# A four-layer hybrid on one core: layer 0's convolution, outputs and query weights rearranged, and a new order at layer 3's end

## The chip, the cores and the metric

The kernel runs on one core of a Trainium2 chip. The core has a matrix engine (TensorE, PE in the profile; its weight loads are listed apart as PEld), VectorE (DVE), ScalarE (ACT), GpSimd (POOL) and SyncE (SP); each works through its own queue in order, and they wait for each other by semaphores. DMA transfers are issued from the queues of SP, ACT and POOL. The metric is the device time of one execution in microseconds (us). All data are float32 unless said otherwise.

## What is computed

An input of 4 images, 256 channels, 32 x 32 pixels goes through four layers. As tokens it is 4 x 1024 rows of 256 numbers. Cut to what matters here, with `B = 4` images, `L = 1024` tokens and `D = 256` channels:

```python
# layer 0: a state-space block with an attention over channels
u = layernorm(x_tokens) * norm_g + norm_b
z, xBC, dt = split(u @ in_w.T);  dt = softplus(dt + dt_bias)
xBC = silu(causal_conv4(xBC) + conv_b);  xs, Bm, Cm = split(xBC)
state_t = state_{t-1} * exp(-dt_t * exp(A_log)) + (dt_t * xs_t) Bm_t;   y_t = state_t Cm_t
y = (y + Dp * xs) * silu(z);  y = y * rsqrt(mean(y*y) + EPS) * rms_w
out = y @ out_w.T                                   # 256 x 256
pooled = mean(out over the image's tokens)
attn = sigmoid(relu(pooled @ se1_w.T + se1_b) @ se2_w.T + se2_b)
x = x + out * attn                                  # attn per image and channel
# layer 1: three 1-channel projections theta, phi, g of x; their product, batch norm, added to x
# layer 2: full attention (one head of 256) over each image, then 2 of 8 experts (256 -> 1024 -> 256)
q = h @ Wq + bq;  k = h @ Wk + bk;  t = t + softmax(q k^T / 16) (h @ Wv + bv)
# layer 3: lam = softmax_tokens(h @ W_k)^T (h @ W_v + b_v), batch norm of lam, t + (h @ W_q + b_q) lam;
#          then an LSTM of 1024 steps over the 4 images; its outputs are added to t
```

silu(v) is v times sigmoid(v), which equals (v/2) (1 + tanh(v/2)).

## The kernel before

The kernel is one program in Bass with the Tile framework. Outside of the blocks `tc.manual_schedule`, the framework's planner chooses the order of the instructions on each engine from the program order and from its own idea of when inputs are ready; so instructions of different images stand among each other in the trace, and some that need only a constant input stand far ahead of their place in the code. `tc.keep_in_program_order(x)` ties an instruction behind the one traced before it on its engine; `tc.issue_after(x)` ties what a block traces on x's engine behind x. Inside a manual block the code's order is the order.

**Layer 0, projection** (`_project`). The tokens come in 8 blocks of 512, two an image. `load` fetches a block, turns it by matmuls with `turner` (L246; the matrix also holds the three weights of layer 1, whose products go to `of_x`), takes the layer norm's moments and scales. `turn` turns it back, `project` multiplies with the weights: z and dt (L276) and the four groups of 128 of xBC, `xbc[b]` (L284, copied by ACT at L287). After an image's second block `convolve(b)` does, for each group `m`, one ACT operation (L294), three DVE multiply-adds of 128x1024 (L299) and a silu on ACT (L302). After the last block `_decays` computes dt and the decay factors of all images: exponent, logarithm, the exponent of A_log (L349), three matmuls with triangular matrices and their exponents (L356). Image 3's `convolve` comes after it. The weights of layer 0 come in one DMA, `w_l0` (in the profile w_l); its part w_out is scaled by rms_w at L201.

**Layer 0, scans** (`_scan`, `_out`). An image has 8 chunks of 128 tokens. A chunk transposes its xBC (ptr, L375), copies it (xb, L378), builds the decay matrix (au L386, pd L388, m_h L390 and L391), multiplies (py L397, pst L406 and L411), updates the state on DVE (L413, L414) and multiplies y with silu(z) into `zs` (L417); ACT sums the squares (L419). `_out(b)` then takes the square root's inverse (rstd, L432, POOL), turns the scaled rows by matmuls with diagonal matrices (L443) into `yT` with sums over tokens (L447), multiplies the sums with w_out (L456), with se1 (L464) and se2 (L468), and takes the sigmoid by tanh (L471). With the attention it scales w_out (`w_att`, L474), gets three more columns by six products summed over channels (`junk`, L478), and multiplies yT with it, chunk by chunk (L486): the 256 columns are added to `s.rows` (L489), the other three go to `of_y` (L490). The code's order is scan 0, scan 1, out 0, scan 2, out 1, scan 3, out 2, out 3. [...]

**Layer 1** (`_layer1`) is a chain of small operations on of_x and of_y, and ends with l1_row (L555). **Layer 2** (`_layer2_attention`) loads its weights w_l2 (L128, also w_l in the profile), folds the query and key weights into one matrix, `m_qk` and `b_qk` (L592 to L602), and then norms image 0's rows (L620, L138, L158), and so on. The experts (`_layer2_experts`) follow; beside the early tiles `_lstm_constants` loads and halves the LSTM's weights (L1474).

**Layer 3's end** (`_layer3_first`, in a manual block). For the first 128 tokens of every image it computes q (L1348, L1353), runs three products that nothing reads (L1360), norms lam (L1416, L1419), multiplies (`p_u`, L1439), adds (L1422), norms, turns (L1434) and copies the result to `u3_first`, the LSTM's first input. Between, `other()` computes products of w_q and lam (`matrices`, L1375) that later tokens need: one of two halves for images 0 to 2. The fourth image's two halves are left to `s.rest[0]`, which `_layer3_lstm` runs in its step t = 0, after that step's own matmuls. A step injects the inputs (L1651), multiplies the state (L1708), and goes through DVE and ACT (L1719 to L1747).

Of the kernel before, what the change touches and what calls it, by code (L numbers as in the profile page):

```python
# [18 lines left out]
P = 128  # L19
B = 4  # L20
# [40 lines left out]
    "norm_g": 2, "norm_b": 2, "conv_w": 16, "conv_b": 4, "rms_w": 2, "se1_b": 1,  # L61
# [64 lines left out]
def _weights(s, name):  # L126
    w = s.wpool.tile([P, C, NW[name]], F32, name=name, tag="w")
    s.nc.scalar.dma_start(w, s.d[name].rearrange("(k p) n -> p k n", p=P))  # L128
    return w
# [40 lines left out]
def _layer0_and_1(s):  # L170
# [5 lines left out]
    with ExitStack() as ctx:  # L176
# [5 lines left out]
        wide = keep.tile([P, 5, D], F32, name="wide")  # L182
        nc.scalar.dma_start(
            wide.rearrange("p i d -> p (i d)"), s.d["wide"].to_broadcast([P, 5 * D])
# [4 lines left out]
            three=wide[:, 2:, :],  # L189
# [10 lines left out]
        for k in range(C):  # L200
            nc.vector.tensor_scalar_mul(  # L201
                v.w_out[:, k, :], v.w_out[:, k, :], s.col["rms_w"][:, k : k + 1]
            )
        _project(s, v, keep)
        v.dt, v.decay, v.total, v.tail = v.decays
        with ExitStack() as body:
            pools = SimpleNamespace(
                scan=body.enter_context(tc.tile_pool(name="ssm", bufs=2)),
                out=body.enter_context(tc.tile_pool(name="out", bufs=2)),
                ps=body.enter_context(tc.tile_pool(name="ssm_ps", bufs=2, space=PSUM)),  # L210
            )
            for b in range(B):
                _scan(s, v, pools, b)
                if b > 0:
                    _out(s, v, pools, b - 1)
            _out(s, v, pools, B - 1)
# [3 lines left out]
def _project(s, v, keep):  # L220
# [4 lines left out]
    with ExitStack() as ctx:  # L225
# [5 lines left out]
        for k in range(C):  # L231
            nc.vector.tensor_copy(turner[:, k, 3:], s.ident)
            for j, name in enumerate(("theta_w", "phi_w", "g_w")):
                nc.vector.tensor_copy(turner[:, k, j : j + 1], s.col[name][:, k : k + 1])
        held = {}
# [53 lines left out]
        def convolve(b):  # L289
            for m in range(NXBC):  # L290
                x = v.xbc[b][:, m, :]
                acc = pool.tile([P, L], F32, name="acc")
                tap = s.col["conv_w"][:, m * DCONV : (m + 1) * DCONV]
                nc.scalar.activation(  # L294
                    acc, x[:, off:], AF.Identity,
                    bias=s.col["conv_b"][:, m : m + 1], scale=tap[:, off:],
                )
                for j in range(off):
                    nc.vector.scalar_tensor_tensor(  # L299
                        acc, x[:, j : j + L], tap[:, j : j + 1], acc, ALU.mult, ALU.add  # L300
                    )
                nc.scalar.activation(x[:, off:], acc, AF.Silu)  # L302
# [4 lines left out]
        for i in range(NBLK):  # L307
# [7 lines left out]
            if i % BPI == BPI - 1:  # L315
                convolve(i // BPI)


def _decays(s, keep, pool, ps, dtr):
# [29 lines left out]
    nc.scalar.activation(na, s.row["A_log"], AF.Exp)  # L349
# [11 lines left out]
def _scan(s, v, pools, b):  # L361
# [5 lines left out]
    state = pool.tile([P, NH, HD], F32, name="state")  # L367
    for c in range(TPI):
        n = b * TPI + c
        t = slice(off + c * P, off + (c + 1) * P)  # L370
        bT, cT = xbc[:, 2, t], xbc[:, 3, t]

        ptr = ps.tile([P, 4, P], F32, name="ptr")
        for m in range(3):
            nc.tensor.transpose(ptr[:, m, :], xbc[:, m, t], s.ident)  # L375
        nc.tensor.matmul(ptr[:, 3, :], bT, cT, start=True, stop=True)
        xb = pool.tile([P, 3, P], F32, name="xb")
        nc.scalar.copy(xb, ptr[:, :3, :])  # L378
        gm = pool.tile([P, P], F32, name="gm")
        nc.vector.tensor_mul(gm, ptr[:, 3, :], s.upper)  # L380
        xh = xb[:, :2, :].rearrange("p c (h d) -> p (c h) d", d=HD)


        au = pool.tile([P, NH, P], F32, name="au")
        for h in range(NH):
            nc.scalar.mul(au[:, h, :], s.upper, a[:, n, h : h + 1])  # L386
        pd = ps.tile([P, NH, P], F32, name="pd", bufs=1)
        nc.tensor.matmul(pd, s.lower, au, start=True, stop=True)  # L388
        m_h = pool.tile([P, NH, P], F32, name="m_h")
        nc.scalar.activation(m_h, pd, AF.Exp)  # L390
        nc.vector.tensor_mul(m_h, m_h, _bc(gm, 1, NH))  # L391

        xdt = pool.tile([P, NH, HD], F32, name="xdt")
        nc.gpsimd.tensor_mul(xdt, xh, _bc(v.dt[:, n, :], 2, HD))
        py = ps.tile([P, NH, HD], F32, name="py", bufs=1)
        for h in range(NH):
            nc.tensor.matmul(py[:, h, :], m_h[:, h, :], xdt[:, h, :], start=True, stop=True)  # L397

        y = pool.tile([P, NH, HD], F32, name="y")
        nc.gpsimd.tensor_mul(y, xh, _bc(s.row["Dp"], 2, HD))  # L400
        nc.vector.tensor_add(y, y, py)
        xw = pool.tile([P, NH, HD], F32, name="xw")
        nc.gpsimd.tensor_mul(xw, xh, _bc(v.tail[:, n, :], 2, HD))
        pst = ps.tile([P, 2, NH, HD], F32, name="pst")
        if c > 0:
            nc.tensor.matmul(pst[:, 0], cT, state, start=True, stop=True)  # L406
            y_in = pool.tile([P, NH, HD], F32, name="y_in")
# [1474 lines left out]
```

## Time and profile before

| | us |
|---|---|
| median of 3 runs | 3427.09 (3426.97 to 3430.27) |
| the profiled execution | 3423.79 |
| its span | 3422.0 |
| layer 0, first matmul to the last of_y | 7.28 to 340.6 |
| layer 1, to l1_row | 340.6 to 348.0 |
| layer 2, attention | 348.0 to about 708 |
| experts | about 708 to 1210 |
| layer 3 to u3_first | about 1240 to 1344 |
| LSTM | 1344 to the end |

All times of single instructions are those of the one profiled execution and count from its span's start. The profile gives, for each engine, busy times, the idle time before an instruction and what ended it ("<-"); a matmul of float32 appears as two passes, so a product over 256 rows of 256 columns is four passes. The chain that ended last is followed back from the last instruction of the program to what released each step.

### The profile page before, as it was taken

Reading aid. Unit: us, or ns where it says so; the run is one execution under the profiler, and the core shown is the slowest. Engines: PE = TensorE matmul, PEld = TensorE weight load, DVE = VectorE, ACT = ScalarE, POOL = GpSimd, SP = SyncE. Lnnn points to the kernel's source line nnn. Section 1 sums busy time; section 2 is a strip of 40 time slices with the busy share of each in tenths; the row PEclk is TensorE's granted clock in tenths of the full one; section 3 lists DMA queues with packets and bytes.
Section 4 is the critical chain, followed back from the end, with each engine's and each line's share of the span. In section 5 each row is a group of like instructions: output and inputs, shape, how many; then the busy total and the mean of one; then the engine's idle time right before and its main releaser. Section 6 shows DMA issues by size and latency. Waiting matters only on the chain.

```text
span 3422.0 us, 143796 instructions
## 1 busy us (share of the span) xinstructions
PE 3104.9 (91%) x63646; PEld 2493.8 (73%) x63646; DVE 1837.6 (54%) x8224; ACT 1099.1 (32%) x4347; POOL 529.4 (15%) x746
## 2 busy tenths in 40 slices
PE   8797899999999989998998998998998998998887
PEld 5476577678888856777777777777777777777776
DVE  5785644651111143565555565555665665555555
ACT  5763222222222222332332332332332332332222
POOL 2252100124444320001001001001001001001000
PEclk9898999999999999999999999999999999999999
DMA  2000011246666620000000000000000000000000
GB/s 82 1 1 1 10 38 38 102 152 213 194 198 210 199 61 1 4 4 10 4 4 10 4 4 10 4 4 10 4 4 10 4 4 10 4 4 9 5 4 10
DMA packets 49220, 140.65 MB, mean 41 GB/s; under 512 B 4944, under 2 KB 38032, under 8 KB 43856
## 3 DMA queue, kind: packets, MB, share of 16 engines
q0 software_dynamic: 18768, 101.03, 9.5%
q1 hardware_dynamic: 27680, 24.45, 2.2%
q8 instruction: 499, 8.18, 1.0%
q10 hardware_dynamic: 2144, 5.95, 0.5%
q14 instruction: 129, 1.06, 0.1%
HBM read 106.18 MB, written 25.22 MB: 38 GB/s over the span
## 4 chain that ended last, share of the span: by engine, by line
PE 54%; DVE 26%; ACT 11%; issue 6%; POOL 2%; DMA 1%; ACTq 0%; DVEq 0%; SPq 0%; POOLq 0%
PE pre L1708 16%; DVE col L1719 11%; PE ph L1204 7%; PE po L1213 7%; PE pre L1651 6%; ACT tri L1722 5%; DVE scan L1731 5%; DVE hs L1742 4%; PE p_a L1605 3%; PE p_w L768 3%; PE p_s L734 3%; DVE acc L299 1%; PE p_o L486 1%; PE p_d L1309 1%; PE p_w L755 1%
## 5 line engine op out<-in xcount | busy, mean ns | idle before, releaser
L1708 PE MATMUL pre<-w_v,hs 128*4 128x64 f32 x49104 | 872.8, 219 | 207.4 <-DVE hs L1742 196.8
L1708 PEld LDWEIGHTS pre<-w_v,hs 128*4 128x4 f32 x49104 | 684.1, 86 | 395.6 <-DVE hs L1742 393.7
L1651 PE MATMUL pre<-xg,pick 128*128 128x64 f32 x6144 | 903.9, 283 | 0.5 <-DVE xg L1618 0.5
L1651 PEld LDWEIGHTS pre<-xg,pick 128*128 128x128 f32 x6144 | 763.5, 191 | 118.1 <-DVE xg L1618 0.9
L1719 DVE STREAM_TRANSPOSE col<-pre 128x64 f32<-128x64 f32 x2048 | 484.0, 250 | 304.2 <-PE pre L1708 289.3
L1722 ACT ACTIVATE tri<-col 128x16 f32<-128x16 f32 x1024 | 229.9, 225 | 1173.5 <-DVE col L1719 1173.5
L1731 DVE TENSOR_TENSOR_SCAN scan<-tri 128x24 f32<-128x24 f32 x1024 | 216.3, 211 | 361.0 <-ACT tri L1722 361.0
L1613 POOL TENSOR_TENSOR xg<-xg,gate_bias 128x192 f32<-128x192 f32 x127 | 75.0, 590 | 1602.9 <-ACT xg L1612 1602.9
L1204 PE MATMUL ph<-xT,wt 128*128 128x256 f32 (+1 forms) x1184 | 253.7, 370 | 1.6 <-issue 0.9
L1207 ACT ACTIVATE hT<-ph,wt 128x256 f32<-128x256 f32 (+1 forms) x296 | 136.9, 463 | 353.6 <-PE ph L1204 346.6
L1213 PE MATMUL po<-wt,hT 128*128 128x256 f32 x1120 | 248.9, 379 | 0.0
L1204 PEld LDWEIGHTS ph<-xT,wt 128*128 128x128 f32 x1184 | 205.6, 189 | 41.6 <-ACT hT L1207 6.2
L1213 PEld LDWEIGHTS po<-wt,hT 128*128 128x128 f32 x1120 | 209.9, 190 | 27.0
L1740 DVE STREAM_TRANSPOSE gate<-row 128x64 f32<-128x64 f32 x1024 | 228.2, 223 | 0.7
L1729 ACT ACTIVATE row<-pre 128x64 f32<-128x64 f32 x1024 | 210.5, 206 | 0.6
L1747 DVE SCALAR_TENSOR_TENSOR tri<-hs,scan 128x8 f32<-128x8 f32 x1023 | 181.6, 178 | 36.1 <-DVE hs L1742 1.5
L1182 DVE COPY xT<-p_x 128x512 f32<-128x512 f32 (+1 forms) x37 | 24.5, 662 | 205.7 <-PE p_x L1178 205.6
L1224 DVE TENSOR_TENSOR y<-po,wt 128x256 f32<-128x256 f32 x70 | 29.6, 424 | 186.0 <-PE po L1213 185.9
L1605 PE MATMUL p_a<-w_u,u 128*32 128x192 f32 x1792 | 119.3, 338 | 0.0
L734 PE MATMUL p_s<-u,q 128*128 128x512 f32 x256 | 117.0, 596 | 0.0
L768 PE MATMUL p_w<-v,prT 128*128 128x256 f32 x512 | 116.0, 379 | 0.7 <-ACT prT L760 0.7
L768 PEld LDWEIGHTS p_w<-v,prT 128*128 128x128 f32 x512 | 95.5, 190 | 15.5 <-issue 2.9
(2462 smaller groups left out, 3284.0 us busy)
## 6 DMA issues: line engine op xcount, KB each, us to landing
xn<-xn SPq DMA_DIRECT2D x8, 516.0 KB, 3.6
x<-in_x_dram SPq DMA_DIRECT2D x16, 256.0 KB, 3.1
acc<-rows SPq DMA_DIRECT2D x8, 512.0 KB, 2.9
out_dram<-part SPq DMA_DIRECT2D x64, 64.0 KB, 1.7
xn_early<-xn SPq DMA_DIRECT2D x6, 516.0 KB, 5.0
rows<-acc SPq DMA_DIRECT2D x6, 512.0 KB, 8.3
w_l<-in_w_l_dram ACTq DMA_DIRECT2D x1, 1092.0 KB, 9.5
rows<-acc SPq DMA_DIRECT2D x4, 256.0 KB, 4.2
```

Source lines behind the costliest of these rows:

```text
L734: nc.tensor.matmul(p[:, h, :], v.q[:, k, bass.ts(j, P)], v.u[:, k, bass.ts(h, W)], start=k == 0, stop=k == C - 1,)
L768: nc.tensor.matmul(p, prT[:, n, :], images[g // TPI].v[:, n, :], start=n == 0, stop=n == TPI - 1)
L1204: nc.tensor.matmul(ph, w1[:, k, bass.ts(m, P)], xT[:, k, :], start=k == 0, stop=k == C - 1)
L1213: nc.tensor.matmul(po, hT[:, m, bass.ts(j, P)], w2[:, m, :], start=m == 0, stop=m == NHC - 1)
L1605: nc.tensor.matmul(p[32 * j : 32 * (j + 1), :], u3[i * SG // P][:, k, bass.ts(i % (P // SG), 32)], w_u[:, k, j * Q : (j + 1) * Q], start=k ...
L1651: nc.tensor.matmul(p, pick[:, r].rearrange("p j r -> p (j r)"), xg[i][:, v], start=True, stop=t == 0,)
L1708: nc.tensor.matmul(p[32 * j : 32 * j + B, :], hs[:, t - 1, k * B : (k + 1) * B], w_v[:, k, j * Q + v.start : j * Q + v.stop], start=False, ...
L1719: nc.vector.transpose(col[:, g * C : (g + 1) * C, :].rearrange("p n r -> p (n r)"), pre[t % 2][g])
L1722: nc.scalar.activation(z[:, 2:50].rearrange("p (g q) -> p g q", g=2)[:, :, ::3].rearrange("p g (k b) -> p (g k) b", k=C), col[:, :, :B], A ...
L1729: nc.scalar.activation(row, pre[t % 2][2], AF.Tanh)
L1731: nc.vector.tensor_tensor_scan(scan, z[:, 0 : 3 * S], z[:, 26 : 26 + 3 * S], 0.0, ALU.mult, ALU.add)
L1740: nc.vector.transpose(gate.rearrange("p n r -> p (n r)"), row)
```

## The change

Layer 0. Image 3's convolution is taken out of `_project` and done in four parts after chunks 0, 2, 4 and 6 of scan 0, with silu as tanh and one more DVE operation; its accumulators have a pool of their own. The scaling of w_out, its transpose `out_t` and the product `w_in` of w_out and se1 are made once, after scan 0's last chunk. `_out` is split: `_attention(b - 1)` is in the code after chunk 1 of scan b, `_out(b - 1, j)` after chunks 4 to 7, two each, and for b = 3 one each. Image 2's other four outputs are tied behind products of image 3's attention. yT lies in xbc[b]'s first two groups. The three columns come from a product of out_t with the theta, phi and g weights times the attention, not from `junk`. w_l2 is loaded after the projection, and m_qk and b_qk are computed at the end of layer 0. The exponent of A_log and L1474's scalings are kept in program order.

Layer 3's end. No products that nothing reads; the second half of q is made by DVE; all four images' lam are scaled first, then the four p_u, then all eight matrices between the adds and the turns; the LSTM's step 0 has no such product any more.

The diff, cut to its core:

```diff
-        for k in range(C):
-            nc.vector.tensor_scalar_mul(
-                v.w_out[:, k, :], v.w_out[:, k, :], s.col["rms_w"][:, k : k + 1])
-        _project(s, v, keep)
-        v.dt, v.decay, v.total, v.tail = v.decays
-        with ExitStack() as body:
...
+        with tc.tile_pool(name="conv", bufs=2, side="right") as conv, ExitStack() as body:
+            _project(s, v, keep, conv)
+            v.dt, v.decay, v.total, v.tail = v.decays
+            s.w_l2 = _weights(s, "w_l2")
+            tc.keep_in_program_order(s.w_load)
...
             for b in range(B):
-                _scan(s, v, pools, b)
-                if b > 0:
-                    _out(s, v, pools, b - 1)
-            _out(s, v, pools, B - 1)
+                for c in range(TPI):
+                    _scan(s, v, pools, b, c)
+                    if b == 0 and c % 2 == 0:
+                        _convolve_last(s, v, pools, conv, c // 2)
+                    if b == 0 and c == TPI - 1:
+                        _out_weights(s, v, pools)
+                    if b > 0 and c == 1:
+                        held = _attention(s, v, pools, b - 1)
+                    if b > 0 and c >= TPI // 2:
+                        n = 1 if b == B - 1 else 2
+                        for j in range(n * (c - TPI // 2), n * (c - TPI // 2 + 1)):
+                            _out(s, v, pools, b - 1, j, held, "p_o")
+            beside = [
+                lambda j=j: _out(s, v, pools, B - 2, j, held, "ptr") for j in range(TPI // 2, TPI)
+            ]
+            last = _attention(s, v, pools, B - 1, beside)
+            for j in range(TPI):
+                _out(s, v, pools, B - 1, j, last, "ptr")
+            _query_weights(s, pools.ps)
...
-            if i % BPI == BPI - 1:
+            if i % BPI == BPI - 1 and i + 1 < NBLK:
                 convolve(i // BPI)
+def _convolve_last(s, v, pools, conv, m):
+    nc = s.nc
+    if m == 0:
...
+        nc.gpsimd.tensor_scalar_mul(v.half_w, s.col["conv_w"], 0.5)
+        nc.gpsimd.tensor_scalar_mul(v.half_b, s.col["conv_b"], 0.5)
+    acc = _convolution(s, v, conv, B - 1, m, v.half_w, v.half_b)
+    dst = v.xbc[B - 1][:, m, DCONV - 1 :]
+    nc.scalar.activation(dst, acc, AF.Tanh)
+    nc.vector.scalar_tensor_tensor(dst, dst, 1.0, acc, ALU.add, ALU.mult)
...
-    nc.scalar.activation(na, s.row["A_log"], AF.Exp)
+    tc.keep_in_program_order(nc.scalar.activation(na, s.row["A_log"], AF.Exp))
...
+def _out_weights(s, v, pools):
+    nc, pool, ps = s.nc, pools.out, pools.ps
+    for k in range(C):
+        s.tc.keep_in_program_order(nc.vector.tensor_scalar_mul(
+            v.w_out[:, k, :], v.w_out[:, k, :], s.col["rms_w"][:, k : k + 1]))
...
+            nc.tensor.transpose(p[:, bass.ts(k, P)], v.w_out[:, k, bass.ts(m, P)], s.ident)
+        nc.scalar.copy(v.out_t[:, m, :], p[:, :D])
...
+def _attention(s, v, pools, b, beside=()):
...
+    def fill(product):
+        if beside:
+            with s.tc.issue_after(product.ins):
+                beside.pop(0)()
...
-    yT = pool.tile([P, C, L], F32, name="yT", bufs=1)
+    yT = v.xbc[b][:, :C, DCONV - 1 :]
...
+    for k in range(C):
+        mm = nc.tensor.matmul(
+            p, v.w_in[:, k, :], pooled[:, k : k + 1], start=k == 0, stop=k == C - 1)
+    fill(mm)
...
+    mine = pool.tile([P, C, 3], F32, name="mine")
+    nc.vector.tensor_mul(mine, v.three, _bc(att[:, D:], 2, 3))
...
-            nc.vector.scalar_tensor_tensor(
-                junk, w[:, k, :D], 1.0, v.three[:, j, :], ALU.mult, ALU.mult,
...
 def _layer3_first
+    p_q = [ps.tile([P, W], F32, name="p_w") for _ in range(C)]
...
-    p = ps.tile([P, W], F32, name="p_w")
-    for _ in range(3):
-        nc.tensor.matmul(p, s.ident, u[:, 0, :W], start=True, stop=True)
...
-    between = [matrices(b, [m]) for b in range(B - 1) for m in range(C)]
+    between = [matrices(b, [m]) for b in range(B) for m in range(C)]
...
     for b in range(B):
         scaled(b)
+        if b == 1:
+            nc.vector.tensor_scalar_add(
+                q[:, 1].rearrange("p b t -> p (b t)"), p_q[1], s.col["b_q"][:, 1:2])
+    for b in range(B):
         for k in range(C):
             nc.tensor.matmul(p_u[b // 2][:, b % 2, :], q[:, k, b, :], lam[:, k, b, :],
...
-        if b < B - 1:
-            other()
-        if b > 0:
-            added(b - 1)
-    normalised(0, B // 2)
-    added(B - 1)
+    added(0)
+    added(1)
+    rstd = _rstd(s, pool, moments[:, : B // 2, :])
+    added(2)
+    _scaled(s, un[:, : B // 2, :], mine[:, : B // 2, :], moments[:, : B // 2, :], rstd)
+    added(3)
     normalised(B // 2, B)
-    other()
-    other()
+    for _ in range(5):
+        other()
...
     turned(0, B // 2)
-    other()
+    for _ in range(3):
+        other()
     turned(B // 2, B)
...
-    s.rest = [matrices(B - 1, list(range(C)))] + [bias(b) for b in range(B)]
+    s.rest = [bias(b) for b in range(B)]
...
-        nc.vector.tensor_scalar_mul(io, io, 0.5)
+        s.tc.keep_in_program_order(nc.vector.tensor_scalar_mul(io, io, 0.5))
...
             if t == 0:
-                p = aside()
-                mm, out = lambda: s.rest[0][0](p), lambda: s.rest[0][1](p)
+                pass
```

`_query_weights` is L592 to L602 of before with two PSUM tiles of the tag p_o; `_convolution` is L294 to L299; `_out` is one chunk of L486 to L490.

## The prediction

> **What bounds the kernel now.** I read the page first, then the windows of layer 0, then the chain that ended last and the timeline in the four places that the diff touches.
>
> The page gives the span, and PE as the fullest engine. The loops that carry the chain (LSTM steps L1708 to L1747, experts L1204 and L1213) aren't edited; they hand any shift on one for one.
>
> ```profile
> span 3422.0 us, 143796 instructions
> PE 3104.9 (91%) x63646; PEld 2493.8 (73%) x63646; DVE 1837.6 (54%) x8224; ACT 1099.1 (32%) x4347; POOL 529.4 (15%) x746
> ```
>
> Windows of layer 0's second half: stretch, length, busy time and count of PE, PEld, DVE, ACT, POOL, then PE clock. The first two are the scans of images 0 and 1 (the py matmuls, eight a chunk, count 71 and 60). PE is the limit with DVE just behind it; in the last row PE works 30 of 43 us at clock 0.76.
>
> ```profile
> 152.00:183.00 31.00, 30.66 (x163) 22.96 (x163) 24.36 (x60) 25.56 (x76) 16.57 (x26) 0.91 0.01 2
> 183.00:213.00 30.00, 27.61 (x158) 20.04 (x158) 28.05 (x64) 21.42 (x65) 20.28 (x29) 1.00 0.00 1
> 260.00:298.00 38.00, 36.17 (x196) 29.32 (x196) 31.27 (x87) 20.25 (x66) 12.67 (x19) 0.91 0.00 1
> 298.00:341.00 43.00, 30.04 (x124) 22.88 (x124) 16.49 (x61) 7.28 (x30) 2.14 (x5) 0.76 0.00 0
> ```
>
> The timeline of the start: DVE, in order, sits on two operations whose DMAs are late (the bias scaling L1474, the w_out scaling L201), and PE waits behind each.
>
> ```profile
> 6.67 0.43 DVE L1474 TENSOR_SCALAR rows<-rows 128x512 f32<-128x512 f32 x1 [2.14 <-DMA rows<-in_rows_dram]
> 7.28 2.12 PE L246 MATMUL p_x<-turner,x 128*128 128x131 f32 x8 [7.28 <-DVE turner L232]
> 11.26 0.62 DVE L201 TENSOR_SCALAR w_l<-w_l,cols 128x256 f32<-128x256 f32 x2 [3.89 <-DMA w_l<-in_w_l_dram]
> ```
>
> The timeline before the first scan: DVE convolves image 3, and the first chunk's xb is copied only at 149.97.
>
> ```profile
> 142.31 6.44 DVE L299 SCALAR_TENSOR_TENSOR acc<-xbc,cols,acc 128x1024 f32<-128x1024 f32 x5
> 149.97 0.48 ACT L378 COPY xb<-ptr 128x384 f32<-128x384 f32 x1
> ```
>
> The chain at the end of layer 0 (start, length): image 2's outputs stand ahead of image 3's turned rows, and its own outputs come after another attention.
>
> ```profile
> 308.51 10.48 PE p_o L486 x32
> 318.99 3.81 PE p_o L443 x32
> 328.67 1.14 DVE junk L478 x6
> 329.94 10.03 PE p_o L486 x32
> ```
>
> The chain at layer 3's end: three filler products (six passes), four rounds of ACT lam then p_u, and after the first LSTM step a product of eight passes that the second step waits for.
>
> ```profile
> 1326.08 2.58 PE p_w L1360 x6
> 1337.27 1.15 PE p_u L1439 x4
> 1343.47 0.59 ACT u_first L1462
> 1348.70 3.52 PE p_a L1375 x8
> 1352.22 0.78 PE pre L1708 x48
> ```
>
> **What the Trainium skill says.** "TensorE: Matmul & The Clock Gate", section "What's actually happening", halves the clock after an idle window of some 3.4 us. The trace agrees: after PE's wait that ended at 308.5 the first passes of L486 come at 0.37 us, later ones at 0.2. "SBUF — State Buffer", section "Who interferes with whom", says that a DVE operation with two SBUF inputs and a GpSimd one that reads SBUF exclude each other. The trace agrees: m_h L391 takes 674 to 1139 ns, and y L409 took 0.83 where POOL's xw ran beside it, else 0.42. "ScalarE: Activation LUTs", section "What ACT_TABLE_LOAD costs", prices a load at 1283 ns; all eight loads before the first chunk show 1.28.
>
> **The change part by part**, in us of the profiled execution (span 3422.0; that run took 3423.79, 1.8 around the span).
>
> 1. *Start.* L1474 and L201 go to later places, and so does the exponent of A_log with a table load (7.04 to 8.53 on ACT). Turner can follow its columns at about 5 instead of 7.28, if x has landed (2.8 us at best from issue at 0.8): −1.5. PE's second stop, 9.4 to 12.0, goes: −2.6. w_l lands at 11.2, ahead of the first p_z (then about 15). From 20 on PE is busy 18 to 19 of every 20 us, so the shift stays: **−4** (−5 to −2). POOL's three new copies run while it is idle (2.6 to 15.4); the w_l2 load costs ACT one issue of 0.38.
>
> 2. *Image 3's convolution moves into scan 0.* The decays then need dtr (125.6), two tables, twelve small DVE operations and three matmuls: about 135, so the chunks start 15 earlier. DVE gets twelve operations of 1.28 in the scan plus four new ones (the product with 1+tanh), also 1.28: 20.5. Against that, scan 0's DVE work is 24 and its PE work 28. Some 4 of the 20.5 fit ahead of 135; the rest makes 24 + 16.5 = 40.5, at about 92% full 44: ends at 179, where scan 0 ends now (about 180). What PE gains at the front it loses to DVE: **0**. Bounds: −12 if the extra work sinks into later DVE gaps; +6 if the shared port stretches it. Tanh beside Exp needs no new load (none shows after 153.18 although L471 is a tanh). Two silu table loads go, inside the 15.
>
> 3. *Scans 1 to 3.* Before 298 PE now also gets image 2's attention (2.2) and four of its outputs (4 x 0.86 = 3.4): 5.6, at 93% full **+6**. The other sixteen outputs were in the scans before. Eight L456 passes (1.05) per image give way to about as many narrow ones; twelve junk operations of 0.35 leave DVE. The w_out scaling and transposition (about 2.5 on PE) fall in scan 0, where DVE is the limit: nothing, 2.5 if that cover is gone. Bounds 0 to +14.
>
> 4. *Tail.* From the last zs (297.2) to the last of_y (340.6) are 43.4 now. After: rstd 3.0; turned rows at first at half clock, about 7, and last yT 0.8; pooled, w_in, hdn 1.2; se2 and two fillers, att, tanh 3.4; mine, out_t and a filler, w_att 2.0; eight outputs at 0.9, 7.2, and 0.8 to the copy: 25.4. **−18** (−22 to −14). Image 2's last four outputs are in it as fillers (0.86 each); if they push each DVE step behind a 0.42 rows add, that is the 14.
>
> 5. *Query weights.* 2.5 of PE at full clock now follow the last output, and layer 1's first matmul is ready 1.3 after of_y: **+0.5** (0 to 1.5). In exchange DVE no longer waits at L602 (350.81) with layer 2's statistics queued behind it: un at about 351 instead of 353.26, **−2.4** (−4 to −1).
>
> 6. *Layer 3's end.* The filler goes (2.58), lam is scaled in one run, and the second q moves from ACT to DVE (0.69). Counted from q's products (end 1326.0): q ready 1326.8, four p_u at 0.86 to 1330.3, eight matrices at 0.86 and 16 transposes (1.0) make 1338.2, and DVE's adds and norms end by 1334.8, under them. Now the last transposes end at 1343.45: **−5.3**.
>
> 7. *First LSTM step.* The eight passes at 1348.70 are among those eight matrices: **−3.5**. Bounds for 6 and 7 together: −10 to −6.
>
> Sum: −4 + 0 + 6 − 18 + 0.5 − 2.4 − 5.3 − 3.5 = −26.7, a span of 3395.3. The median of the runs shown, 3427.09, stands 5.1 above the span; 3427.1 − 26.7 = **3400**.
>
> **The rivals.**
> - *DVE isn't the limit in scan 0*: the convolution fills DVE's gaps over two scans (31 of 77 us from 183 to 260 aren't all filled: PE and DVE both leave some 6). Against it: it is issued among image 0's chunks, in order. Item 2 becomes −12: 3388.
> - *Denser scans than PE can use*: the port exclusion and 2 outputs per chunk spoil the order, items 2 and 3 go to their upper ends, +6 and +14, less a little: 3411. For it: DVE at 28 of 30 us with POOL at 20 in the second row of windows.
> - *Slower*: every in-scan output and yT group takes one of two p_o buffers, and PE, in order, stands at it until DVE's add and ACT's copy come up in queues full of scan work. 20 outputs and 12 groups are 32 such stops; at 0.84 each the whole gain is gone, at 1.2 the time is 3438. Against it: in the scans before, 32 passes of image 0's outputs took 7.8 with chunks between them, and the waits for of_y came to 3.0 in nine.
> - *The change does nothing there*: layer 0 returns what it gains at the tail (image 3's chain as long as before, since the four fillers sit in it), and only items 6 and 7 with their bound remain, with a scan loss: 3423.
>
> **How the numbers follow.** Chances: forecast 0.50 (own range 3393 to 3406), fuller scans 0.17, denser scans 0.24, no net effect 0.05, slower 0.04. 3385 to 3413 takes the forecast's cases and most of the next two, about 0.82. About 0.2% (6.9 us) is what a measurement of this kernel can tell from no change: faster 0.91, same 0.05, slower 0.04.
>
> **What would show it.** PE's first p_x at about 5 with no stop near 10 (item 1). First xb copy near 131 in the new time, and PE with gaps in scan 0 while DVE is over 90% busy (2). The last zs some 2 us after today's 297 (3). About 25 from there to the last of_y, with L486's counterpart in groups of four between the attention's products (4). No p_q products after layer 1's (5). u3_first copied 16 after the first q product and not 21 (6), LSTM's second step right after the inject (7). I am wrong if scan 0 takes much over 45 us, if PE stalls before p_y in the scans, or if the experts' stage (100% PE from 760 to 1200) changes length, which I take as fixed.

## The result, and the profile after

The changed kernel takes **3416.92 us** (median of seven runs, 3414.05 to 3419.39) against 3426.97 (3425.33 to 3430.27): ratio **0.9969, 95% interval 0.9957 to 0.9981**. That is 10 us faster, not 27: below the kernel before, and above the forecast's range (3385 to 3413). The two profiled executions lie only 4.4 apart (3423.79 and 3419.39), so differences of 2 or 3 us over their long later stages are not read. How far two executions of the same code can differ shows in a version told below that keeps layer 0 of the kernel before, in the same order on every engine: its profiled execution ends layer 0 at 336.87, that of the kernel before at 340.44. And from the second LSTM step's products to the end, where no version differs, the profiled executions of all fifteen take from 2069.4 to 2075.4.

Line numbers below are those of the changed kernel unless said otherwise: taps of image 3's convolution L340, xb L421, pd L431, m_h L433 (ACT) and L434 (DVE), zs L460, rstd L507, diag L514, turned rows L518, outputs L575.

The page's head, of the changed kernel: TensorE is as full as before, over a span 4.4 shorter.

```profile
span 3417.6 us, 143837 instructions
PE 3108.0 (91%) x63668; PEld 2496.8 (73%) x63668; DVE 1838.2 (54%) x8185; ACT 1095.4 (32%) x4351; POOL 536.1 (16%) x751
```

Windows of layer 0's second half, changed kernel: stretch, length, busy time and count of PE, PEld, DVE, ACT, POOL, then PE clock (and last the share and GB/s of DMA). The rows are scan 0, scan 1, scan 2, scan 3 and the tail.

```profile
132.00:184.00 52.00, 39.84 (x166) 25.36 (x165) 45.22 (x75) 35.93 (x90) 26.12 (x29) 0.83 0.04 15
184.00:231.00 47.00, 42.19 (x237) 32.53 (x236) 35.36 (x87) 25.89 (x86) 20.18 (x29) 0.96 0.00 1
231.00:278.00 47.00, 41.85 (x230) 33.55 (x230) 31.87 (x82) 25.50 (x84) 17.48 (x27) 0.93 0.00 1
278.00:315.00 37.00, 33.58 (x198) 27.39 (x198) 28.22 (x75) 18.71 (x60) 12.71 (x20) 0.95 0.00 1
315.00:341.00 26.00, 21.38 (x105) 18.16 (x106) 8.77 (x28) 6.28 (x26) 2.13 (x4) 0.87 0.00 1
```

Scan 0 has grown to 52 us with TensorE 77% busy, at clock 0.83, and VectorE at 45 of 52. The tail has shrunk from 43 to 26. In the scans after it TensorE stands at 89 to 91%, where the kernel before had 92 and 95%.

Timeline of the changed kernel, the start and the first chunk (start, length, engine, line, and in brackets the idle time before it and what ended it):

```profile
4.69 0.80 PE L266 MATMUL p_x<-turner,x 128*128 128x131 f32 x2 [4.69 <-DVE turner L250]
6.50 1.65 PE L266 MATMUL p_x<-turner,x 128*128 128x131 f32 x6 [1.01 <-DMA x<-in_x_dram]
8.91 4.86 PE L266 MATMUL p_x<-turner,x 128*128 128x131 f32 x20 [0.77 <-DVE of_x L270]
...
132.27 0.48 ACT L421 COPY xb<-ptr 128x384 f32<-128x384 f32 x1 [1.48 <-PE ptr L419]
```

TensorE begins 2.6 earlier, its stop behind of_x is 0.8 instead of 2.6 (a new one of 1.0 waits for x itself), and the first xb comes 17.7 earlier than before (149.97). But scan 1's first m_h comes at 183.84, where it came at 181.34. What happens between is in the chain of scan 0, changed kernel (start, length, what):

```profile
152.84 2.07 PE pd L431 x2
...
160.57 1.09 PE py L440 x8
...
161.76 0.42 DVE y L444
162.18 1.20 DVE acc L340
163.37 0.75 DVE y L452
164.13 0.33 DVE state L457
164.46 0.42 DVE zs L460
164.88 1.20 DVE acc L340
166.07 0.20 DVE gm L423
166.28 0.06 DVE acc L340
166.33 1.22 issue
167.55 0.69 DVE m_h L434
...
168.37 1.94 PE py L440 x8
```

The taps stand in VectorE's queue between a chunk's own steps, and the m_h that TensorE needs for py comes after three of them. TensorE, with holes, falls to half clock again and again: py's eight passes take 1.09 before this stretch and 1.94 after it, and pd's two passes 2.07, at full clock (225.55, below) 1.02.

Timeline at the boundary of scans 1 and 2, changed kernel:

```profile
225.55 1.02 PE L431 MATMUL pd<-au,lower 128*128 128x512 f32 x2
...
228.51 1.64 POOL L507 TENSOR_TENSOR rstd<-rstd,power 128x8 f32<-128x8 f32 x1
...
230.18 1.20 DVE L514 TENSOR_SCALAR diag<-ident,rstd 128x128 f32<-128x128 f32 x2 [3.55 <-POOL rstd L507]
...
231.29 1.12 DVE L434 TENSOR_TENSOR m_h<-m_h,gm 128x512 f32<-128x512 f32 x1
...
232.56 0.66 PE L440 MATMUL py<-xdt,m_h 128*128 128x64 f32 x2 [2.81 <-DVE m_h L434]
```

The planner put image 1's first diagonals ahead of scan 2's first m_h on VectorE. Their rstd is not there yet: GpSimd first serves the new chunk (xdt, y, xw), and the power takes 1.64. VectorE stands 3.55, m_h waits behind it, and TensorE stands 2.81. The same stop of 3.55 is at 277.1, and one of 1.18 at 191.1. The kernel before has one of 0.29 and one of 3.55, ahead of scan 3's first m_h:

```profile
257.91 1.76 DVE L439 TENSOR_SCALAR diag<-ident,rstd 128x128 f32<-128x128 f32 x3 [3.55 <-POOL rstd L432]
```

The chain at the tail and at layer 3's end, changed kernel:

```profile
318.60 6.38 PE p_o L518 x32
...
332.83 7.31 PE p_y L575 x32
...
1325.09 3.71 PE p_w L1436 x8
...
1329.72 3.26 PE p_u L1527 x14
1332.98 4.32 PE p_d L1458 x20
...
1340.74 0.50 ACT u_first L1551
...
1345.17 0.85 PE pre L1796 x48
```

At the tail one group of outputs stands in the chain, not two. At layer 3's end the fillers are gone, the eight small matrices stand together (20 and 12 passes around four transposes), and the second step's products (pre) follow u_first by 4.4 instead of 8.8.

Boundaries of the stages in the profiled executions. The last two columns are experiments told below: diagonals pinned, and image 3's convolution moved to scans 1 and 2.

| | before | changed | pinned | convolution later |
|---|---|---|---|---|
| decays' first table load | 126.61 | 122.38 | 122.36 | 122.50 |
| first xb | 149.97 | 132.27 | 131.91 | 131.51 |
| scan 1's first m_h | 181.34 | 183.84 | 181.42 | 161.89 |
| last zs | 296.78 | 314.81 | 303.55 | 289.30 |
| last of_y | 340.44 | 340.88 | 329.03 | 314.34 |
| u_first | 1343.47 | 1340.74 | 1327.96 | 1312.77 |
| second step's pre | 1352.22 | 1345.17 | 1332.39 | 1317.19 |
| median of the runs | 3426.97 | 3416.92 | 3409.24 | 3393.00 |

The last of_y, where layer 0 ends, has not moved. Layer 0's start and tail gained 4.2 and 17.6; scan 0 gave back 6.7 and scans 1 to 3 gave back 15.5.

### The profile page after: what moved, and what is told of

Its sections match the earlier page's. It is cut to its first block, busy times and chain, and to the rows that moved or that the text cites. A ratio compares the mean times of both kernels' runs of the same rounds, so it can differ in the third digit from the quotient of the medians.

```text
span 3417.6 us, 143837 instructions
## 1 busy us (share of the span) xinstructions
PE 3108.0 (91%) x63668; PEld 2496.8 (73%) x63668; DVE 1838.2 (54%) x8185; ACT 1095.4 (32%) x4351; POOL 536.1 (16%) x751
## 4 chain that ended last, share of the span: by engine, by line
PE 55%; DVE 26%; ACT 11%; issue 6%; POOL 2%; DMA 1%; ACTq 0%; DVEq 0%; SPq 0%; POOLq 0%
PE pre L1796 16%; DVE col L1807 11%; PE ph L1292 7%; PE po L1301 7%; PE pre L1740 6%; ACT tri L1810 5%; DVE scan L1819 5%; DVE hs L1830 4%; PE p_a L1694 3%; PE p_w L856 3%; PE p_s L822 3%; DVE acc L340 1%; PE py L440 1%; PE p_d L1397 1%; PE p_k L1365 1%
## 5 line engine op out<-in xcount | busy, mean ns | idle before, releaser
L1270 DVE COPY xT<-p_x 128x512 f32<-128x512 f32 (+1 forms) x37 | 24.5, 663 | 205.8 <-PE p_x L1266 205.6
L856 PEld LDWEIGHTS p_w<-v,prT 128*128 128x128 f32 x512 | 95.5, 190 | 15.5 <-issue 2.9
```

The costliest lines, as they stand in the source:

```text
L856: nc.tensor.matmul(p, prT[:, n, :], images[g // TPI].v[:, n, :], start=n == 0, stop=n == TPI - 1)
```

## The experiments

Times against the kernel before are against its median in the same group of runs: 3426.12 for the first three sections, 3425.72 for the two after them, 3428.03 for the rest and 3426.66 for the very last run. In brackets stand the ratio to it and its 95% interval.

### Layer 3's end alone, and layer 0 alone

The first takes the kernel before and gives it `_layer3_first` as changed, with `s.rest` of biases alone and nothing in step 0. The second takes the changed kernel and puts those back.

> The kernel before with only the new order at layer 3's end (q's second half on VectorE, all eight small matrices between the products, nothing of them left for the recurrence's first step); layer 0 is untouched. Theory A, 'the rearranged layer 0 is worth nothing, all of the gain is layer 3's': 9 to 10 us under the kernel before, so 3417 to 3418, as the traces' -5.4 (last transposes) and -4.4 (second step of the recurrence) say. Rival B, 'the recurrence gives part of it back, and layer 0 has a share': at most 5 us under, 3422 or more.

> The changed kernel with layer 3's end as it was: layer 0 and the query weights alone are rearranged. Theory A: within 1 us of the kernel before, 3426 to 3428. Rival B: some 5 us under it, 3422. The forecast's own working (items 1 to 5) would have 18 us under it, 3409.

Measured: layer 3 alone **3417.18**, 8.9 under before (0.9973, 0.9962 to 0.9985). Layer 0 alone **3426.95**, 0.8 above (1.0000, 0.9992 to 1.0009). Theory A holds on both sides: all that the change gained is layer 3's, and the rearranged layer 0 is worth nothing as it stands. The question is what eats the 22 us that its start and tail gain.

### Image 3's convolution back in the projection

```diff
-            if i % BPI == BPI - 1 and i + 1 < NBLK:
+            if i % BPI == BPI - 1:
                 convolve(i // BPI)
...
-                    if b == 0 and c % 2 == 0:
-                        _convolve_last(s, v, pools, conv, c // 2)
```

> The changed kernel, but image 3 is convolved in the projection as the other three are, with Silu; all else as changed. Theory C, 'scan 0 is held by VectorE, which the moved convolution fills (45 us busy of the 52 before scan 1)': scan 0 begins some 13 us later than in the changed kernel but takes half the time, scan 1's first m_h comes at 178 to 180 instead of 183.8, and the kernel is 4 to 6 us under the changed one, 3411 to 3413. Rival D, 'what the scans ask of TensorE sets the time, wherever the convolution is': within 1.5 us of the changed one, 3415.5 to 3418.5.

Measured: **3425.68** (0.9994 of before, 0.9986 to 1.0003), and scan 1's first m_h not at 178 to 180 but at 190.55. Theory C missed: scan 0 ends 6.7 later than in the changed kernel, not earlier. Its runs spread from 3419.13 to 3429.91, and the profiled one, the 3419.13, ends layer 0 at 340.81, as the changed kernel does; why the median lies 9 above the changed kernel's isn't settled. Windows of this version:

```profile
130.00:143.00 13.00, 3.75 (x15) 3.22 (x16) 7.95 (x11) 10.79 (x13) 0.00 (x0) 0.50 0.00 1
143.00:152.00 9.00, 3.54 (x7) 1.49 (x6) 8.54 (x8) 3.81 (x12) 8.14 (x6) 0.50 0.01 3
152.00:160.00 8.00, 6.98 (x17) 4.09 (x18) 1.77 (x4) 5.33 (x9) 0.05 (x1) 0.50 0.29 99
```

For 30 us TensorE is at half clock. From 142.3 to 151.0 VectorE works through the convolution's last six taps, and the first gm stands behind them; in the stretch before it is busy only 8 of 13 us, in the one after 2 of 8. Its timeline there:

```profile
142.32 8.69 DVE L338 SCALAR_TENSOR_TENSOR acc<-xbc,cols,acc 128x1024 f32<-128x1024 f32 x6 [0.84 <-ACT acc L334]
...
146.79 1.59 POOL L444 TENSOR_TENSOR xw<-xb,tail 128x256 f32<-128x256 f32 x1
...
150.93 0.28 DVE L421 TENSOR_TENSOR gm<-ptr,upper 128x128 f32<-128x128 f32 x1
```

ScalarE has a part as well, since silu is back: its function tables are loaded nine times from 122.6 to 162.8, where the changed kernel has three loads from 122.4 to 126.1. Image 3's last two silus lie inside scan 0, behind the load at 155.06, and the one at 162.75 stands ahead of an m_h. So VectorE's share of the trouble isn't refuted by this run, nor shown by it: scan 0 takes 38.5 us from its first m_h to scan 1's (24.5 in the kernel before), and what share each engine has in that isn't separated.

### The diagonals pinned behind the second chunk

```diff
-    nc.vector.tensor_mul(m_h, m_h, _bc(gm, 1, NH))
+    v.weighed = nc.vector.tensor_mul(m_h, m_h, _bc(gm, 1, NH))
...
-            nc.vector.tensor_scalar_mul(diag[:, j, :], s.ident, rstd[:, n : n + 1])
+            with s.tc.issue_after(v.weighed.ins):
+                nc.vector.tensor_scalar_mul(diag[:, j, :], s.ident, rstd[:, n : n + 1])
```

> The changed kernel, with the diagonals of images 0 to 2 queued on VectorE behind the second chunk's m_h of the scan that they lie in, so that VectorE doesn't stand at GpSimd's rstd ahead of a scan's first m_h. Theory E, 'this in-order wait is on the path': the stalls of 3.55, 2.4 and 1.2 us go, and the kernel is 4 to 7 us under the changed one, 3410 to 3413. Rival D, 'TensorE has too much to do in the scans, and the stall is caught up within a chunk': within 1.5 us of the changed one, 3415.5 to 3418.5.

(The stops in the trace are 3.55, 3.55 and 1.18, not 3.55, 2.4 and 1.2.) Measured: **3409.24**, 7.7 under the changed kernel (0.9948 of before, 0.9934 to 0.9962). Theory E: both stops of 3.55 are gone, and that of 1.18 stays. The scans' windows of this version:

```profile
131.90:181.40 49.50, 37.42 (x165) 23.68 (x163) 44.85 (x74) 35.62 (x90) 25.97 (x29) 0.88 0.04 15
181.40:303.60 122.20, 114.24 (x665) 90.02 (x665) 94.03 (x243) 70.14 (x228) 51.27 (x74) 0.99 0.00 1
```

Scans 1 to 3 take 122.2 instead of 131.0, with the same 665 passes. TensorE's idle time falls from 13.2 to 8.0, and its busy time from 117.8 to 114.2, since its clock goes from 0.95 to 0.99.

### The attention as filler again, and the pin in the kernel before

The first writes `_attention` and the outputs of image b-1 after the whole of scan b:

```diff
-                    if b > 0 and c == 1:
-                        held = _attention(s, v, pools, b - 1)
...
+                if b > 0:
+                    held = _attention(s, v, pools, b - 1)
+                    for j in range(TPI if b < B - 1 else TPI // 2):
+                        _out(s, v, pools, b - 1, j, held, "p_o")
```

> The changed kernel with the attention and output products of image b-1 written after the whole of scan b, as the kernel before had them, instead of inside it from its second chunk on (the first four outputs of image 2 still ahead of image 3's attention); the tail is as changed. A second way to get the diagonals out from in front of a scan's first m_h: the built order has them behind it in scans 1 and 2. Theory E, 'the in-order wait at rstd is what the scans lost': as good as with the diagonals pinned, 3408 to 3413. Rival H, 'pinning paid by something else, and work placed in the code's order packs TensorE better than filler': within 1.5 us of the changed kernel or above it, 3415.5 or more.

The second pins the kernel before's diagonals in the same way, behind the second m_h of the scan after their image.

> The kernel before, nothing changed but that the diagonals of images 0 to 2 are queued on VectorE behind the second m_h of the scan that follows their image. Its trace shows one full stop of 3.55 us at rstd (at 257.9, ahead of scan 3's first m_h) and one of 0.29. Theory E prices a stop at about what it lasts: 3 to 4 us under the kernel before, 3422 to 3423. Rival I, 'the stop is hidden there, since TensorE is full anyway': within 1 us, 3425 to 3427.

Measured: filler **3406.73** (0.9948, 0.9934 to 0.9962), as good as the pin, which is theory E's outcome and not rival H's. But it is no clean second way to it. Stops of 0.97, 0.64 and 2.64 stay in its scans, 4.3 us of the changed kernel's 8.3, and more of the work falls into the tail: scans 1 to 3 have 630 passes in 114.5 us, and the tail takes 36.3 instead of 26.1. Its longest stop:

```profile
252.01 1.19 DVE L512 TENSOR_SCALAR diag<-ident,rstd 128x128 f32<-128x128 f32 x2 [2.64 <-POOL rstd L505]
```

The pin in the kernel before: **3419.04**, 6.7 under it (0.9981, 0.9974 to 0.9988), about twice the 3 to 4 expected of its one stop of 3.55. Windows of scans 1 to 3, first of the kernel before, then of it with the pin:

```profile
181.30:296.80 115.50, 108.22 (x620) 84.45 (x619) 96.84 (x254) 70.17 (x222) 55.26 (x76) 0.97 0.00 1
```

```profile
182.00:292.40 110.40, 105.04 (x621) 81.98 (x619) 96.80 (x254) 69.80 (x222) 53.48 (x76) 1.00 0.00 1
```

Of the 5.1 that the scans become shorter, 1.9 are TensorE's idle time and 3.2 its busy time for as many passes, at clock 1.00 instead of 0.97. Against the second trace of the same layer 0 (the version with layer 3's end alone) it is 3.6: 1.9 of idle time and 1.7 of busy time. The tail is 4.5 shorter too (43.6 to 39.1; 2.9 against the second trace), in an order that the planner changed with the pin; the windows name no single cause. This corrects the reading of the pin: it is worth about the same in both kernels (6.7 and 7.7). So the stops are not what separates the two, and can't alone be what ate layer 0's gain.

### What holds scan 0: VectorE or TensorE's clock

Both stand on the pinned version. One leaves out two of image 3's three taps, so it computes less; the other adds products that nothing reads.

```diff
-    for j in range(off):
+    for j in range(off if b < B - 1 else 1):
```

```diff
+    mm = nc.tensor.matmul(pd, s.lower, au, start=True, stop=True)
+    if b == 0 and c < TPI - 1:
+        p = ps.tile([P, W], F32, name="p_o")
+        with s.tc.issue_after(mm.ins):
+            nc.tensor.matmul(p, s.ident, v.w_xbc[:, 0, :], start=True, stop=True)
```

> The changed kernel with pinned diagonals, and of image 3's convolution two of the three taps on VectorE are left out (its values are then not the reference's): eight instructions of 1.34 us, 10.7 us of VectorE less in scan 0. Theory F, 'VectorE holds scan 0': scan 1's first m_h comes 7 to 10 us earlier than with pinned diagonals alone (181.4), and the kernel takes 3399 to 3403. Rival G, 'the chain over TensorE at its low clock holds scan 0': at most 2 us earlier, 3407 to 3410.

> The changed kernel with pinned diagonals, and in scan 0 seven more 128x512 products that nothing reads, one behind each chunk's pd product (about 1.0 us each at full clock), to keep TensorE's granted clock up (0.88 there now). Rival G: the clock goes to 0.95 or more and scan 1's first m_h comes 2 to 4 us earlier, 3405 to 3407. Theory F: TensorE isn't what scan 0 waits for; between 0 and 3 us later, 3409 to 3412.

Measured: without the taps **3394.52** (0.9913 of before, 0.9898 to 0.9928), 14.7 under the pinned version and more than the 6 to 10 expected; layer 0's end, 10.6 earlier, accounts for that much, and the rest isn't explained. Scan 1's first m_h comes at 170.51, 10.9 earlier for 10.7 us of VectorE. With the extra products **3409.03** (0.9958, 0.9943 to 0.9973), no different from the pinned version, and scan 1's first m_h at 182.39, 1.0 later. Theory F: VectorE holds scan 0, one for one. Scan 0 without the two taps, then with the extra products:

```profile
131.90:170.50 38.60, 31.82 (x154) 20.65 (x152) 34.44 (x66) 33.18 (x85) 22.32 (x27) 0.97 0.06 20
```

```profile
131.90:182.40 50.50, 42.11 (x175) 26.61 (x174) 45.57 (x76) 35.25 (x89) 26.10 (x29) 0.91 0.04 15
```

TensorE's clock comes back by itself (0.97) once VectorE keeps up; feeding it idle products raised it from 0.88 to only 0.91 and moved nothing. Since the products didn't reach the 0.95 that rival G asked for, and the missing taps raised the clock along with what they saved, the clock as a part of the cause is not excluded by these two runs; the sum in VectorE's time, 10.9 for 10.7, leaves it little room.

### The two gains of the kernel before together

> The kernel before with two edits that each stood alone in an earlier run: the diagonals pinned behind the second m_h (-6.7 there), and the new order at layer 3's end (-8.9 there). Layer 0 is otherwise as before. Theory J, 'the stops cost both kernels about alike, and layer 0's rearrangement is worth nothing with or without them': the two add, 15 to 16 us under the kernel before, 3410 to 3411, level with the changed kernel with pinned diagonals (3409.2). Theory K, 'the stops ate what the rearrangement had gained': 5 us or more above the changed kernel with pinned diagonals, 3414 or more.

Measured: **3414.21** (0.9957, 0.9943 to 0.9970), 13.8 under before, with runs from 3406.19 to 3414.97. As it stands this is 5.0 above the pinned changed kernel, where theory K begins; each against the kernel before of its own group (13.8 and 16.9 under) it is 3.1, between the theories, and the runs of the two overlap (the pinned ones go from 3404.09 to 3411.98). So the time doesn't tell J and K apart. In the profiled execution, its fastest run, layer 0 ends at 331.35, the pinned changed kernel's at 329.03, and 2.3 is less than the 3.6 by which one and the same layer 0 differed. With the pin on both sides the rearranged layer 0 is worth 2 to 5 us, and how much of that is noise stays open.

### Image 3's convolution elsewhere

All on the pinned version, except the second on the filler version; the last is the kernel before with this part alone. (The third text below was on record behind the first, and "the run before this one" in it is the first.) The edit, here with four blocks in scans 1 and 2:

```diff
+            v.pieces = [(1, 0), (1, 4), (2, 0), (2, 4)]
...
-                    if b == 0 and c % 2 == 0:
-                        _convolve_last(s, v, pools, conv, c // 2)
+                    if (b, c) in v.pieces:
+                        _convolve_last(s, v, pools, conv, v.pieces.index((b, c)))
```

> The changed kernel with pinned diagonals, and image 3's convolution cut over three scans: two of its four blocks in scan 0 (chunks 0 and 4), one in scan 1 and one in scan 2 (chunk 4 of each). All is computed. Theory F, 'VectorE holds scan 0 and TensorE the later scans': scan 0 loses 10.3 us of VectorE, scan 1's first m_h comes 8 to 10 us earlier (172), and scans 1 and 2, where VectorE is busy 34 of 43, take the blocks for 1 us each at most: 3399 to 3403. Rival L, 'the later scans have no room on VectorE either (the shared port, PE waiting for m_h)': what scan 0 gains they lose, 3407 to 3410.

> The cut convolution of the run before the last (two blocks in scan 0, one each in scans 1 and 2) on the version that writes an image's attention and outputs after the next scan (3406.7 alone). Theory F: the two gains add, 3397 to 3401. Rival L: 3405 to 3408.

> As the run before this one, but all four blocks of image 3's convolution lie in scans 1 and 2 (chunks 0 and 4 of each), none in scan 0. Theory F: scan 0 takes what it took in the kernel before, some 31 us from its first xb, and scan 1's first m_h comes at 163 to 166; scans 1 and 2 get 10.3 us of VectorE each, on 34 of 43, and end some 3 us later each: 3395 to 3402. Rival L: scans 1 and 2 become VectorE's and take 6 to 8 us longer each, 3404 to 3410.

> The kernel before with one part of the change alone, but put elsewhere: image 3's convolution leaves the projection and lies in scans 1 and 2, two blocks each (Tanh form, half weights), and the turned rows lie in xbc to make room; start, attention, tail and layer 3's end as before. Theory M, 'the convolution's place decides, whatever else is rearranged': the stretch from the decays to the first chunk loses some 14 us and the later scans give 4 to 6 back, 3414 to 3419, against 3427; with layer 3's 8.9 that leaves 12 to 17 of the 34 us of the best version for the start and the tail. Rival N, 'the early first chunk is only worth something together with the new tail': at most 4 us under the kernel before, 3423 or more.

Measured:

| | us | ratio to before | scan 1's first m_h | last of_y |
|---|---|---|---|---|
| two blocks in scan 0, one each in 1 and 2 | 3397.92 | 0.9914 (0.9900 to 0.9927) | 175.23 | 320.31 |
| the same, attention as filler | 3410.02 | 0.9945 (0.9931 to 0.9958) | 174.11 | 326.47 |
| two blocks each in scans 1 and 2 | **3393.00** | 0.9897 (0.9882 to 0.9913) | 161.89 | 314.34 |
| kernel before, two blocks each in 1 and 2 | 3430.18 | 1.0005 (0.9999 to 1.0012) | 165.76 | 339.32 |

Moving the convolution two scans on makes the best version, 35 us under the kernel before and 24 under the changed one. Windows of its scan 0, scans 1 to 3 and tail:

```profile
131.50:161.90 30.40, 29.45 (x163) 21.27 (x162) 26.16 (x60) 27.11 (x80) 20.04 (x29) 1.00 0.08 26
161.90:289.30 127.40, 116.08 (x668) 89.83 (x666) 109.49 (x257) 79.22 (x239) 58.16 (x74) 0.99 0.00 1
289.30:314.30 25.00, 20.20 (x104) 16.92 (x105) 8.95 (x28) 6.12 (x25) 2.12 (x4) 0.93 0.00 1
```

Scan 0 has TensorE at 97% and full clock, in 30.4 us. The later scans take 5.2 longer than pinned alone, for 15.5 us more VectorE work. The stops at rstd in the scans go with it but for one of 0.86, and the pins have no part in that: with the pins left out this version is the same program, instruction for instruction on every engine. So one edit of the changed kernel, the blocks' places, makes the 24 us.

The last row is the miss: 3.5 above the kernel before where theory M had 8 to 13 under it. Its windows from the first xb:

```profile
136.00:167.00 31.00, 29.66 (x154) 20.89 (x154) 25.95 (x57) 24.66 (x73) 20.01 (x27) 0.95 0.01 1
167.00:290.00 123.00, 105.90 (x551) 77.52 (x551) 107.78 (x248) 72.27 (x213) 56.09 (x69) 0.93 0.00 1
```

Scan 1 starts 15.6 earlier than before, and by the last zs (300.01, before 296.78) all of it is lost: TensorE is busy 86% at clock 0.93. Rival N: the place pays only together with the rest. Layer 0 ends where it ended before (339.32), so the 3.5 us above aren't explained by it. What in the rest makes the difference isn't settled. A candidate is the `junk` products, which the change drops (24 of them took 9.5 us of VectorE after 160 in the kernel before); no run varied them, and TensorE's waits in these scans name them for 1.6 us only, against 5.9 for gm and 7.8 for m_h. Nor is it settled why cutting the convolution gains 11 on the pinned version and nothing on the filler one. In the traces it does gain there too: layer 0 ends 5.6 earlier (332.11 to 326.47), and 3.4 of that go in the recurrence (2075.4 from the second step's products to the end, against 2071.9), which isn't edited.

## Why the prediction was wrong

By its own items, from the profiled executions:

1. *Start* (−4): **right**. The decays' first table load comes 4.2 earlier.
2. *Image 3's convolution into scan 0* (0): **wrong, this is the first step that failed**. From that table load to scan 1's first m_h passed 54.7, and now pass 61.5: +6.7, just over the bound of +6 that was named. The item had found the right limit (VectorE) and sized it low: 40.5 us of work, at 92% full 44 long; measured 45.1 in 51.6, 87% full. It added up VectorE's work as if any order would do; in the queue the taps stand ahead of m_h, and TensorE runs its passes at a mean clock of 0.83. How much of the lost fill is the order's, no run separates.
3. *Scans 1 to 3* (+6, bounds 0 to +14): **wrong, the second failed step**: 115.5 became 131.0, +15.5. TensorE's busy time grew by 9.6, where 5.6 was reckoned. Its groups of passes show where: sixteen more passes of outputs (5.3 by the sum of their rows), the attention's small products (7.8 against 4.3), and w_out's transposition and product with se1 (1.8), which the item put under VectorE's cover in scan 0 and which ran in scan 1. (One image's attention more lies in this stretch; the other groups together are 1.0 less.) Idle time grew by another 5.9, to which the stops at rstd belong (pinned, 5.2 of it goes), and the text had none of them, although the kernel before shows one of 3.55.
4. *Tail* (−18): **right**, 43.7 to 26.1 (−17.6).
5. *Query weights* (+0.5 and −2.4): right in sign and size, +0.7 and −1.9.
6. *Layer 3's end* (−5.3): **right**, 21.1 to 15.7 from q's first product to the end of the last transposes (−5.4).
7. *First step* (−3.5): right, a little small, −4.4 from there to the second step's products.

With the measured terms: −4.2 + 6.7 + 15.5 − 17.6 + 0.7 − 1.9 − 5.4 − 4.4 = −10.6, against −10.05 by the medians. So two of the terms made the error, 6.7 and 9.5 us of it. A second pair of traces, layer 3's end alone against layer 0 alone, repeats layer 0's terms: −3.9, +7.2, +15.5 and −16.8. The profiled pair shows only 4.4 of the gain: it loses 2.9 between the experts and layer 3's first product, and 2.6 in the recurrence, where the diff changes nothing, and which the medians don't show.

Of the rivals, "denser scans" (3411, 0.24) had the place and too small a size; "the change does nothing in layer 0" (3423, 0.05) had the outcome, but the tail did give its gain, and the scans took it. Its 0.05 was the misjudgment among the chances. "Slower, p_o stalls" was not seen: TensorE's waits in scans 1 to 3 of the changed kernel name m_h (7.3), xw (4.4) and the state (0.4), no output. "VectorE isn't the limit in scan 0" (3388) came near the right price for another place: with the convolution spread over scans 1 and 2 the kernel takes 3393, less than the forecast's 3400. Here a reading went wrong that mattered: from 183 to 260 VectorE is busy 64.4 of the 77 us, so 12.6 were free, not the 6 that the prediction names against this rival. Three more readings differ from the trace and change no term by much: scan 0's TensorE work was 29.5, not 28; from 20 on TensorE is busy 17 to 19 of every 20 us; and at the tail the clock was at 0.50 from 304 on, after an idle stretch of 3.65 that ended at 300.81, so before the wait that ended at 308.5, with L486's first passes 0.43 apart and later ones 0.22.

Two statements of the Trainium skill reach further than they were used. "SBUF — State Buffer", section "Who interferes with whom", was priced at up to +6 on VectorE alone; GpSimd pays too: xw takes 0.61 at 227.53 in the changed kernel, and 1.59 beside the taps in the version with the convolution back. "TensorE: Matmul & The Clock Gate", section "What's actually happening", was used for the tail and not for scan 0; and there the trace says more than that section's idle window of some 3.4 us: between 160.6 and 168.4 TensorE's records show no idle time over 1.3 us at a stretch, and py's passes still fell to half speed.

## What to carry to other kernels

Before moving work under a stage, ask whether the engine that does it has room there, and whether its in-order queue lets the stage's own steps go first; look for the instruction on the critical path that will stand behind it. A gain at the front and the end of a pipelined stage is kept only if the middle can absorb the moved work: add up each engine's busy time per stage before and after. When a rearrangement brings nothing, try the moved piece in a third place before going back: here two scans later was 24 us better than the new place, though the same place in the kernel before brought nothing.

## What the runs showed of the hardware

Queuing the diagonals of the kernel before behind m_h, which took out one stop of 3.55 us on VectorE and changed the tail's order too, made it 6.7 us faster; in its scans as many passes (620, 619 and 621) kept TensorE busy 108.2 and 106.8 in two traces with the stop and 105.0 without. TensorE fell to half clock in scan 0 without one idle stretch over 1.3 us (its eight py passes from 1.08 to 1.94). In scan 0 seven products that nothing reads brought TensorE's granted clock only from 0.88 to 0.91, and no time; with the convolution moved away, and the holes with it, it was 1.00. A power of 128x8 on GpSimd took 1.64 us, nearly three times a product of 128x256 there (0.61).
